# A six-stage graph network on one core: turned-row copies that also read a late weight, and one product issued a step later

## Chip, core and metric

One core of a Trainium2 chip runs the whole kernel. The metric is the device time of one execution in microseconds (us). The matrix engine is called PE, its weight loads PEld, the vector engine DVE, the scalar engine ACT, the general-purpose engine POOL, and SP issues the transfers (DMA).

## The reference, cut to what matters

Input is `x` (3327 x 256) and a 0/1 matrix `adj` (3327 x 3327). Six masked softmax attentions follow one another; each later one reads the rows of the one before.

```python
x = _layernorm(x + L0(x, adj))        # cosine attention          -> layer "0"
x = _layernorm(x + L1(x, adj))        # GAT, elu                  -> layer "1"
x = _layernorm(x + L2(x, adj))        # query-key attention, elu  -> layer "2"
h = x @ W0                            # L3: three GAT layers      -> "3a", "3b", "3c"
h = _gat_layer(h, adj, W1, a1); h = _gat_layer(h, adj, W2, a2); h = _gat_layer(h, adj, W3, a3)
x = _layernorm(x + h)

def _gat_layer(h, adj, W, a):
    Wh = h @ W
    e = jax.nn.leaky_relu(Wh @ a[:F] + (Wh @ a[F:]).T, ALPHA)
    att = jax.nn.softmax(jnp.where(adj > 0, e, NEG_INF), axis=1)
    return jax.nn.elu(att @ Wh)
```

The kernel multiplies the attention weights by `h` first and by `W` afterwards, so each finished block of rows has to be turned (transposed) and multiplied by a 256 x 256 matrix.

## The kernel before, in words

Rows are cut into 26 tiles of 128 (`NT = 26`). Queries are handled in seven blocks: blocks 0 to 5 hold 512 rows (four tiles), and block 6 holds only 256 (two tiles). Block 6 is called the half-wide block here, and block 5 is `b == NB - 2`, the one in front of it.

The main loop runs over layers, blocks and 26 steps `j`. A step takes one tile of weights `e` (128 keys x 512 or 256 queries), which ACT and DVE made some steps earlier (`Gat.weights`, L657 and L668; five buffers hold `e`), and multiplies it with the 128 x 257 rows of values, once for each tile `k` of the block: `po[k] += e[:, k]' * V[j]` (L1405; in the last block of layer 3c, L1390). `po` are PSUM banks, five in all, of which a full block uses four and a half-wide block two. So the fourth tile of block 0 takes the bank in which tile 0 of the half-wide block before was summed, and its first product cannot start before ACT has read that bank (L1026).

The rows of a finished block are completed by the generator `finish(L, b, pos)`, advanced one stage in each step of the next block. In the GAT layers it scales the rows (L1022, L1025 on DVE, L1026 on ACT) and calls `turn`: ACT splits the float rows into 16-bit planes (L834), a transposing DMA writes `turned` (L837), the generator then yields `turn_steps(L, b)` times, and DVE copies the two halves back into float order as `pT4` (two 128 x 1024 16-bit copies for a block of four tiles, L844). In block 5 each tile of `pT4` is then multiplied by the layer's matrix (`pproj`, L1062), followed by elu on ACT and DVE (L1075 to L1091). Block 5 is finished while the half-wide block runs.

Engines work through their own instructions in order. The order is written by hand only in the first four steps; afterwards a scheduler orders each engine's instructions, starting from the program's order. A yield more in a generator therefore moves the instructions after it by a step or less, or not at all.

In the last block of layer 3c (`end` in the loop) the two tiles are done one after the other, all 26 products of the first and then of the second; `finish_last` completes each (L1204 to L1256), while `finish` of block 5 runs beside it (its normalised rows `o4`, L1118, and their stores, L1128). After the last product there is one more `finish_last` chain on PE, ACT and DVE, and a store.

Of the kernel before, what the change touches and what calls it, by code (L numbers as in the profile page):

```python
# [8 lines left out]
F32 = mybir.dt.float32  # L9
# [5 lines left out]
ALU = mybir.AluOpType  # L15
# [4 lines left out]
P = 128  # L20
# [13 lines left out]
def gnn_stack(ctx: ExitStack, tc: tile.TileContext, a: dict, N: int, out: bass.AP):  # L34
# [8 lines left out]
    nc = tc.nc  # L43
    NT = (N + P - 1) // P
    NP = NT * P
    NB = (NP + CH - 1) // CH
# [6 lines left out]
    def tiles_of(b):  # L53
        return range(4 * b, min(4 * b + 4, NT))
# [4 lines left out]
    cols = ctx.enter_context(tc.tile_pool(name="cols", bufs=2))  # L59
# [6 lines left out]
    def bank(name):  # L66
# [4 lines left out]
    start = tc.manual_schedule(  # L71
        engines={engines.PE, engines.Activation, engines.DVE, engines.Pool}
    )
# [9 lines left out]
    n = 8  # L83
# [9 lines left out]
    for k in range(4):  # L93
# [5 lines left out]
    V = [  # L99
        [big.tile([P, D + 1], F32, name=f"v{i}_{t}") for t in range(NT)]  # L100
        for i in range(2)
    ]
# [195 lines left out]
    def load_x(g):  # L298
        for t in tiles_of(g):
            nc.sync.dma_start(V[0][t][:, :D], a["x"][t * P : (t + 1) * P, :])  # L300
# [382 lines left out]
    def strassen(L, b):  # L683
        return L.key == "2" or (L.key == "0" and 0 < b < NB - 1)
# [139 lines left out]
        return z[:, : 2 * q]  # L824


    def turn(x4, n, out, steps=3):

        half = "p k (n t) -> p t k n"
        pl = work.tile([P, 4, 2, D], U16, tag="x4k", name="planes", bufs=2)
        for t in range(2):
            nc.scalar.copy(pl[:, :n, t, :], x4[:, :n, :].bitcast(U16).rearrange(half, t=2)[:, t])  # L834
        yield
        tr = work.tile([P, 16, P], U16, tag="stage", name="turned", bufs=4)
        nc.sync.dma_start_transpose(  # L837
            out=tr[:, : 4 * n, :], in_=pl[:, :n].rearrange("p k t n -> p (k t n)")
        )
        for _ in range(steps):  # L840
            yield
        trv = tr[:, : 4 * n, :].rearrange("p (k t h) i -> p t k h i", t=2, h=2)
        for t in range(2):
            nc.vector.tensor_copy(out(t), trv[:, t])  # L844
        yield

    def turn_steps(L, b):

        if L.key == "1":
            return 5 if b == NB - 2 else 3  # L850
        return 7 if b == NB - 2 else 4

# [79 lines left out]
    def finish(L, b, pos):  # L934
# [4 lines left out]
        n = len(ts_)  # L939
# [71 lines left out]
        else:  # L1011
# [15 lines left out]
            if L.key in x_d:  # L1027
                x4 = work.tile([P, 4, D], F32, tag="stage", name="x4", bufs=4)
# [6 lines left out]
            es, pTs = {}, {}  # L1035

            if L.key != "2":
                pT4 = work.tile([P, 4, 2, P], F32, tag="x4k", name="pT4", bufs=2)
                yield from turn(
                    p4,  # L1040
                    n,
                    lambda t: pT4[:, :n].bitcast(U16).rearrange(
                        "p k h (i t) -> p t k h i", t=2
                    )[:, t],
                    turn_steps(L, b),
                )
                pTs = {k: pT4[:, k] for k in range(n)}
                if b < NB - 2:
                    c4 = work.tile([P, 4, D], F32, tag="x4k", name="c4", bufs=2)
                    yield from projected4(pT4, w[L.w], c4)  # L1050
# [55 lines left out]
        if not L.hidden:  # L1106
# [29 lines left out]
            if L.key == "1":  # L1136
# [8 lines left out]
                for k, t in enumerate(ts_):  # L1145
                    pm = bank("pv")
                    for h in range(2):
# [4 lines left out]
                            start=(h == 0),  # L1152
                            stop=(h == 1),
# [122 lines left out]
    def advance():  # L1276
        while pending:
            try:
                next(pending[0])
                return  # L1280
            except StopIteration:
                pending.popleft()
# [8 lines left out]
    steps = [(L, b, j) for L in layers for b in range(NB) for j in range(NT)]  # L1291
    made = deque()
# [45 lines left out]
    def make_to(n):  # L1338
        nonlocal upto
        while upto < n:  # L1340
            make(upto)
            upto += 1

    for s, (L, b, j) in enumerate(steps):
        last = L.key == "3c"
        end = last and b == NB - 1

        if last and b == NB - 2 and j > 10:
            extra += 1
        first = L.key == "0" and b == 0  # L1350
        if j == 0:
            wo, no = (CH, 4) if strassen(L, b) else (D + 1, len(tiles_of(b)))
            pos = [ps_o.tile([P, wo], F32, tag="po", name="po") for _ in range(no)]
        if first:

            if j == 0:
                load_x(1)
                load_xT(2)
            elif j % 4 == 2 and j < 20:
                load_x((j + 6) // 4)  # L1360
            elif j % 4 == 3 and j < 16:
                load_xT((j + 9) // 4)
        make_to(s + LA + 1 + extra)
        if first:
            if j < 2:
                next(q1)
                if j == 1:
                    next(q1, None)
            elif j == 2 or j % 4 == 1 and j < 18:
                prep = keys0(max(2, (j + 7) // 4))  # L1370
            next(prep, None)
            if j == 4:
                next(prep, None)
        if L.key == "0" and b < NB - 1:

            at = 10 if b == 0 else 3
            if j == at:
                load_xT(b + 1)
            elif j == at + 3:
                kprep = queries0(b + 1)  # L1380
            if j >= at + 3:
                next(kprep, None)
        es = None if end else made.popleft()
        if es is not None:
            gate[0] = es[0] if isinstance(es, tuple) else es
        if end:

            k, h = divmod(2 * j, NT)
            for i in (h, h + 1):
                nc.tensor.matmul(  # L1390
                    pos[k],
                    made[i][:, k * P : (k + 1) * P],
                    V[1][i],
                    start=(i == 0),
                    stop=(i == NT - 1),
                )
            if j == 0:
                xm = fetch_last()
            if j == NT // 2 - 1:
                ends.append(finish_last(pos[0], xm, 0))  # L1400
            if ends:
                next(ends[0], None)
        elif not strassen(L, b):
            for k in range(len(pos)):
                nc.tensor.matmul(  # L1405
                    pos[k],
                    es[:, k * P : (k + 1) * P],
                    V[L.i % 2][j],
                    start=(j == 0),
                    stop=(j == NT - 1),  # L1410
                )
        elif j % 2:
            products(pos, b, j // 2, es, V[L.i % 2])
        if s == 3:
            start.__exit__(None, None, None)
        if L.key == "0" and j == NT - 1 - LA:
            sum_adj(b)
        if first and 9 <= j < 18:
            combine("0", j - 6, V[0], es)
        elif first and 20 <= j < 24:  # L1420
            combine("0", (j - 21) % (NT // 2), V[0], es)
        advance()
        if L.key == "0" and b < NB - 1:
            if j == 8:
                masks[b + 1] = new_mask(b + 1)
        elif j == 8 and not (last and b == NB - 1):
            nb = (b + 1) % NB
            masks[nb] = fetch_mask(nb)
        if (b, j) == (1, 0):

            if L.key == "1":
                setup = setup3("3b", 2, "w_l0_wqk")
            elif L.key == "3a":
                setup = setup3("3c", 3, "w_l1_w")
        if b >= 1 and j % 3 == 1:
            next(setup, None)
        nl, nb = (L, b + 1)
        if nb == NB:
            nl, nb = (None if last else layers[L.i + 1]), 0
        begin = 2 if last and b == NB - 2 else 14  # L1440
        if L.is_gat and (b, j) == (0, 22):
            sum_weights(w[L.w])
        if j == (25 if L.key == "1" else 22) and not end:
            while pending:
                advance()
        if nl is not None and nl.key != "0":
            if j == begin:
                pre = ahead(nl, nb)
            if j >= begin:
                next(pre, None)  # L1450
        if j == NT - 1:
            if b == 0 and not last:
                nl = layers[L.i + 1]
                L.sum = Sum()
                if nl.is_gat:
                    if nl.key == "1":
                        while "row_1" not in w:
                            next(setup)
                    nl.gat = Gat(nl.key)
                    L.gat_next = nl.gat  # L1460
            if end:
                pending.append(finish_last(pos[1], xm, 1))
            else:
                pending.append(finish(L, b, pos))
            advance()
# [65 lines left out]
```

## Time and profile before

| | |
|---|---|
| median of three runs | 2361.19 us (2360.8 to 2361.67) |
| the profiled execution | 2362.33 us, of which the span is 2360.6 us |
| PE busy | 2336.8 us, 99% of the span |
| DVE busy | 1661.3 us, 70% |
| ACT busy | 1222.2 us, 52% |
| chain that ended last | PE 94%, DVE 3%, ACT 1%, DMA 1% |

The chain is the sequence of work that released the last instruction, followed backwards. A share of 94% for PE means that the time is PE's own work, together with what PE had to wait for. An idle DVE or ACT costs nothing in itself.

### The profile page before, as it was taken

The page shows a single profiled execution, that of the slowest core. Times are in us where ns is not written, and L with a number is a line of the kernel's source. Part 1 is how long each engine was busy: PE and PEld are TensorE (multiplying, and loading weights), DVE is VectorE, ACT ScalarE, POOL GpSimd, SP SyncE. Part 2 cuts the span into 40 slices and gives each one's busy share as a digit, 9 for nine tenths or more (in the row PEclk, how much of TensorE's full clock was granted, in tenths as well). Part 3 has the DMA queues.
Part 4 walks back from the last instruction along what each step waited for, and adds up shares of the span by engine and source line. Part 5 has one row for each costly group of instructions (what it writes and reads, how often), then busy time and mean ns, then how long its engine had stood idle before and what let it go on. Part 6 is the DMA issues. An engine that isn't in the chain of part 4 may idle for free.

```text
span 2360.6 us, 33869 instructions
## 1 busy us (share of the span) xinstructions
PE 2336.8 (99%) x12205; PEld 1916.7 (81%) x12205; DVE 1661.3 (70%) x4481; ACT 1222.2 (52%) x1979; POOL 38.2 (2%) x156
## 2 busy tenths in 40 slices
PE   9999999999999999999999999999999999999997
PEld 7788888888888777767767798888888888888886
DVE  7789999867777667566566686666656666666675
ACT  4667777755555422222222255555655555655554
POOL 0000001000000000000000000000000000000000
PEclk9999999999999999999999999999999999999998
DMA  8655566423222322212212221211211111132211
GB/s 274 187 190 185 171 196 193 151 74 83 74 84 60 104 54 88 79 54 88 74 50 73 81 86 50 74 52 26 76 47 43 43 60 52 43 98 70 61 51 39
DMA packets 147292, 214.71 MB, mean 91 GB/s; under 512 B 76093, under 2 KB 101172, under 8 KB 142516
## 3 DMA queue, kind: packets, MB, share of 16 engines
q1 hardware_dynamic: 146852, 212.28, 29.4%
q8 instruction: 96, 1.57, 0.3%
q14 instruction: 72, 0.59, 0.1%
q10 hardware_dynamic: 272, 0.26, 0.0%
HBM read 167.53 MB, written 28.19 MB: 83 GB/s over the span
## 4 chain that ended last, share of the span: by engine, by line
PE 94%; DVE 3%; ACT 1%; DMA 1%; issue 1%; POOL 0%; POOLq 0%; SPq 0%; DVEq 0%
PE po L1405 48%; PE po L779 20%; PE ps L563 12%; PE ps L492 6%; PE pproj L890 3%; PE pv L1148 1%; PE pgq L522 1%; ACT re L657 1%; DMA turned<-planes 1%; PE po L1390 1%; PE pk L353 1%; PE pq L317 0%; DVE e L668 0%; PE pproj L1062 0%; DVE v L668 0%
## 5 line engine op out<-in xcount | busy, mean ns | idle before, releaser
L1405 PE MATMUL po<-v,e 128*128 128x257 f32 x5616 | 1248.6, 381 | 1.5 <-ACT p L1026 1.3
L1405 PEld LDWEIGHTS po<-v,e 128*128 128x128 f32 x5616 | 1057.7, 190 | 165.3 <-issue 9.3
L657 ACT ACTIVATE re<-u,nrh,th 128x512 f32<-128x512 f32 (+1 forms) x728 | 555.4, 780 | 486.7 <-DVE e L668 481.0
L668 DVE SCALAR_TENSOR_TENSOR e<-re,rh,mask 128x512 f32<-128x512 f32 (+1 forms) x702 | 500.9, 718 | 333.6 <-PE po L1405 282.5
L563 PE MATMUL ps<-gT,ft 128*128 128x512 f32 (+1 forms) x728 | 307.4, 563 | 0.0
L571 ACT ACTIVATE ex<-ps,off 128x512 f32<-128x512 f32 (+1 forms) x182 | 119.1, 656 | 356.2 <-PE ps L563 354.5
L779 PE MATMUL po<-tsums,ssum 128*128 128x128 f32 (+1 forms) x1794 | 249.3, 275 | 0.0
L477 DVE SCALAR_TENSOR_TENSOR e<-ex,mask 128x512 f32<-128x512 f32 (+1 forms) x182 | 118.6, 652 | 163.5 <-ACT ex L571 162.6
L779 PEld LDWEIGHTS po<-tsums,ssum 128*128 128x128 f32 x1794 | 224.5, 192 | 0.7 <-ACT y L982 0.3
L563 PEld LDWEIGHTS ps<-gT,ft 128*128 128x128 f32 x728 | 132.0, 190 | 114.5 <-issue 111.7
L779 PEld LDWEIGHTS po<-v,e 128*128 128x128 f32 x1196 | 169.3, 191 | 67.2 <-issue 53.1
L779 PE MATMUL po<-v,e 128*128 128x129 f32 x1196 | 182.3, 275 | 0.0
L505 ACT ACTIVATE ex<-ps,rq 128x512 f32<-128x512 f32 (+1 forms) x183 | 118.9, 652 | 117.6 <-PE ps L492 107.7
L492 PE MATMUL ps<-ft,ft 128*128 128x512 f32 (+1 forms) x312 | 142.5, 561 | 0.0
L506 DVE SCALAR_TENSOR_TENSOR e<-ex,mask 128x512 f32<-128x512 f32 (+1 forms) x183 | 116.9, 644 | 33.6 <-ACT ex L505 32.7
L449 DVE CUSTOM_DVE_ANT_0 acc<-acc,stage 128x1024 uint16<-128x1024 uint16 (+1 forms) x168 | 108.8, 648 | 12.2 <-DMA stage<-in_adj_a 8.8
L779 PE MATMUL po<-v,ssum 128*128 128x128 f32 x598 | 92.2, 275 | 0.0
L779 PE MATMUL po<-tsums,e 128*128 128x128 f32 x598 | 92.1, 275 | 0.0
L436 ACT ACTIVATE mask<-pos 128x1024 uint8<-128x1024 bf16 (+1 forms) x87 | 86.3, 992 | 2.1
L435 ACT ACTIVATE pos<-stage 128x1024 bf16<-128x1024 int32 (+1 forms) x87 | 85.6, 983 | 1.2 <-DVE e L506 1.2
L779 PEld LDWEIGHTS po<-v,ssum 128*128 128x128 f32 x598 | 79.4, 192 | 0.1
L779 PEld LDWEIGHTS po<-tsums,e 128*128 128x128 f32 x598 | 79.3, 192 | 0.0
(290 smaller groups left out, 1895.2 us busy)
## 6 DMA issues: line engine op xcount, KB each, us to landing
mask<-mask_d SPq DMA_DIRECT2D x30, 1664.0 KB
stage<-in_adj_a SPq DMA_DIRECT2D x78, 512.0 KB
tsums<-t_d SPq DMA_DIRECT2D x152, 256.5 KB
mask_d<-mask SPq DMA_DIRECT2D x6, 1664.0 KB
u<-s_d SPq DMA_DIRECT2D x24, 256.0 KB
xT<-in_xT SPq DMA_DIRECT2D x10, 512.0 KB
mask<-mask_d SPq DMA_DIRECT2D x5, 832.0 KB
t_d<-tsums SPq DMA_DIRECT2D x14, 256.5 KB
```

The costliest lines, as they stand in the source:

```text
L436: nc.scalar.activation(mask(b, j, 2), t_[:, : 2 * wd], AF.Sign)
L449: nc.vector.tensor_tensor(acc, acc, st[:, h * wd : (h + 1) * wd], ALU.add)
L477: nc.vector.scalar_tensor_tensor(e[:, :wd], t_[:, :wd], 0.0, mask(b, j), ALU.add, ALU.mult)
L492: nc.tensor.matmul(ps[:, :wd], FT[j // 4][:, 0, (j % 4) * P : (j % 4 + 1) * P], FT[b][:, 1, :wd], start=True, stop=True,)
L505: nc.scalar.activation(t_[:, c], ps[:, c], AF.Exp, scale=rq[:, j : j + 1])
L506: nc.vector.scalar_tensor_tensor(e[:, c], t_[:, c], 0.0, mask(b, j)[:, c], ALU.add, ALU.mult)
L563: nc.tensor.matmul(ps[:, :wd], FT[j // 4][:, h, (j % 4) * P : (j % 4 + 1) * P], g[:, h, :wd], start=(h == 0), stop=(h == 1),)
L571: nc.scalar.activation(t_[:, :wd], ps[:, :wd], AF.Exp, bias=off, scale=1.0 / D**0.5)
L657: nc.scalar.activation(t_[:, :wd], self.u[b][:, :wd], AF.Relu, bias=self.nrh[:, j : j + 1], scale=self.th[:, j : j + 1],)
L668: nc.vector.scalar_tensor_tensor(e[:, :wd], t_[:, :wd], self.rh[:, j : j + 1], mask(b, j), ALU.add, ALU.mult,)
L779: nc.tensor.matmul(o, x, y, start=(p == 0 and g not in banks[:i]), stop=(p == NT // 2 - 1 and g not in banks[i + 1 :]),)
L1405: nc.tensor.matmul(pos[k], es[:, k * P : (k + 1) * P], V[L.i % 2][j], start=(j == 0), stop=(j == NT - 1),)
```

## The change

Two things are changed.

First, in `turn`, when it is called for `pT4` of block 5 in layers 1, 3a and 3b (`late`), the two copies become additions of a per-partition value `nought`, which is 0 and is computed from the newest weights tile that exists. The copies thereby depend on those weights. The number of yields ahead of the copies goes from 5 to 6 in layer 1 and from 7 to 9 in layer 3c; it stays 7 in 3a and 3b. Layer 3c keeps plain copies.

Second, in block 0 of layers 3b and 3c, the first product of the fourth tile (step 0) is issued in step 1, between the third and the fourth product of that step.

```diff
-    def turn(x4, n, out, steps=3):
+    def turn(x4, n, out, steps=3, late=False):
...
         trv = tr[:, : 4 * n, :].rearrange("p (k t h) i -> p t k h i", t=2, h=2)
-        for t in range(2):
-            nc.vector.tensor_copy(out(t), trv[:, t])
+        if late:
+
+            e = next(m for m in reversed(made) if m is not None)
+            nought = cols.tile([P, 1], F32, tag="nought", name="nought")
+            nc.vector.tensor_scalar(nought, e[:, :1], 0.0, None, ALU.is_lt)
+            for t in range(2):
+                nc.vector.tensor_scalar(out(t), trv[:, t], nought, None, ALU.add)
+        else:
+            for t in range(2):
+                nc.vector.tensor_copy(out(t), trv[:, t])
         yield
     def turn_steps(L, b):
         if L.key == "1":
-            return 5 if b == NB - 2 else 3
-        return 7 if b == NB - 2 else 4
+            return 6 if b == NB - 2 else 3
+        if b == NB - 2:
+            return 9 if L.key == "3c" else 7
+        return 4
...
                     turn_steps(L, b),
+                    b == NB - 2 and L.key != "3c",
                 )
...
         elif not strassen(L, b):
-            for k in range(len(pos)):
+            todo = [(es, j, k) for k in range(len(pos))]
+
+            if L.key in ("3b", "3c") and b == 0:
+                if j == 0:
+                    held = todo.pop()
+                elif j == 1:
+                    todo.insert(3, held)
+            for e, i, k in todo:
                 nc.tensor.matmul(
                     pos[k],
-                    es[:, k * P : (k + 1) * P],
-                    V[L.i % 2][j],
-                    start=(j == 0),
-                    stop=(j == NT - 1),
+                    e[:, k * P : (k + 1) * P],
+                    V[L.i % 2][i],
+                    start=(i == 0),
+                    stop=(i == NT - 1),
                 )
```

In the order of instructions that the scheduler makes of the changed program, each engine's row of instructions is the old one with these differences:

- Layers 1, 3a and 3b, DVE: the two copies stand where they stood, behind the weights tile of step 12. `nought` stands two or three weights tiles ahead of them. Of the elu work behind them, the first operation comes one weights tile later.
- Layers 1, 3a and 3b, PE: the first `pproj` stands where it stood, between the two products of step 10. In layer 1 the second `pproj` now comes behind the second product of step 10 instead of in front of it, and the third and fourth come one step later. In 3a and 3b nothing moves.
- Layer 3c, last block, PE: each `pproj` of block 5 comes four products later: the first behind product 23 of the first tile instead of product 19, the fourth behind product 9 of the second tile instead of product 5, and so behind the projection of `finish_last` for the first tile. ACT and DVE follow; the four `o4` and their stores come behind the store of the first `olast`.
- Block 0 of 3b and 3c, PE: the held product moves as written. ACT: the `u` of the next block (L649) comes ahead of two `re` (L657) instead of behind them.

## The prediction

> **What bounds the kernel now.** I read the page first: busy time and the chain that ended last.
>
> ```profile
> PE 2336.8 (99%) x12205; PEld 1916.7 (81%) x12205; DVE 1661.3 (70%) x4481; ACT 1222.2 (52%) x1979; POOL 38.2 (2%) x156
> PE 94%; DVE 3%; ACT 1%; DMA 1%; issue 1%; POOL 0%; POOLq 0%; SPq 0%; DVEq 0%
> ```
>
> PE is idle for only 2360.6 - 2336.8 = 23.8 us. The change takes away no product, so it can win only from that idle time. Next come PE's waits (line waited for: us in total, times, longest).
>
> ```profile
> PE pproj L1062 <- DVE pT L844: 4.8, 4, 1.5
> PE pasum L464 <- DVE af L460: 2.0, 2, 1.6
> PE po L1405 <- ACT p L1026: 1.3, 2, 0.7
> ```
>
> The change touches the first and the third row. In the timeline of PE the four waits on pT are 0.71 us (layer 1, before 786.42), 1.05 (3a, before 1689.96), 1.54 (3b, before 2008.74) and 1.50 (3c, before 2326.50). Those on p are 0.66 (block 0 of 3b) and 0.65 (block 0 of 3c). Together 6.1 us. Another 13.2 us lie behind the last product work (PE ends at 2347.4), where the last rows are completed and stored.
>
> What ends the waits on pT is seen in the timeline of 3b, and of 3c:
>
> ```profile
> 2007.33 1.35 DVE L844 COPY pT<-turned 128x1024 uint16<-128x1024 uint16 x2 [1.70 <-DMA turned<-planes]
> ...
> 2008.74 1.13 PE L1062 MATMUL pproj<-w_l_w,pT 128*128 128x256 f32 x4 [1.53 <-DVE pT L844]
> ...
> 2325.00 1.35 DVE L844 COPY pT<-turned 128x1024 uint16<-128x1024 uint16 x2 [1.79 <-DMA turned<-planes]
> 2326.50 1.10 PE L1062 MATMUL pproj<-w_l_w,pT 128*128 128x256 f32 x4 [1.50 <-DVE pT L844]
> ```
>
> DVE stands before the copies and waits for the transposing DMA (1.70 and 1.79 us; 0.87 in layer 1, 1.20 in 3a). The copies then take 1.35, and PE follows within 0.15 us. So two things set the end of this wait: when the DMA lands, and how long the copies last. The change alters the second and leaves the first. The rows that price copies, by shape (busy us, mean ns of one | idle before):
>
> ```profile
> L844 DVE COPY pT<-turned 128x1024 uint16<-128x1024 uint16 x48 | 32.9, 740 | 17.9 <-DMA turned<-planes 17.9
> L1118 DVE TENSOR_SCALAR v<-y,st,rstd 128x256 f32<-128x256 f32 x52 | 18.3, 409 | 0.3
> L1079 DVE TENSOR_SCALAR z<-c 128x256 f32<-128x256 f32 x40 | 9.0, 288 | 0.3
> L432 DVE TENSOR_SCALAR mask<-stage 128x1024 uint8<-128x1024 int32 x4 | 2.7, 686 | 0.0
> L537 DVE TENSOR_REDUCE gm<-gT 128x2 f32<-128x1024 f32 x6 | 7.3, 1219 | 13.9 <-ACT gT L529 13.9
> ```
>
> L1079 and L1118 handle the same 128x256 floats in SBUF. The one with a constant takes 288 ns, the one with per-partition scalars 409: 121 ns more for 256 elements, 0.47 ns an element.
>
> **Held product, 3b and 3c.** Before, the fourth tile's first product waits until ACT has read the bank. Now three products of step 1 go ahead of it: PE runs took 6.66 us for 30 such instructions and 4.93 us for 22, so a product (two instructions) costs 1.73 / 4 = 0.43 us and three 1.29 us, against waits of 0.66 and 0.65. Both waits go: -1.3 us. What covers it is the weights tile of step 1, which must exist; DVE's weights wait mostly for PE to free a buffer (the row below), so they run ahead. The tile of step 0 is released 1.3 us later, and with five buffers its successor is wanted only about four steps (6.9 us) on.
>
> ```profile
> DVE e L668 <- PE po L1405: 282.5, 345, 1.4
> ```
>
> The `u` of the next block, now two `re` earlier on ACT, delays those by its 0.70 us. Its DMA was issued at 1702.30 and it would run at about 1711.9, 9.6 us later, where the transposes landed within 4 to 5; the weights behind have the slack just named. Cost 0.
>
> **Tail, layer 3c.** The first `pproj` stands four products later, 1.72 us of PE work. PE reaches it at 2325.00 + 1.72 = 2326.72, and pT is complete at 2326.35. The wait of 1.50 us goes. What is late next? The fourth `pproj` used to start at 2334.59. Counting PE's work up to product 9 (2338.04 before, less 1.50, less one `pproj` of 0.86), it now starts at 2335.7. That is 1.1 us later, and all of block 5's normalisation follows on DVE, queued ahead of the second `plast` copy (L1204) that starts the last chain. Before, DVE needed from that tile's L1082 (2336.06) to the end of `olast` (2343.46) 7.40 us; of this, L1229 to L1234 (0.48 + 0.42 + 0.42 + 0.43) now run earlier, so DVE is free at about 2337.2 + 5.65 = 2342.9. PE's last product ends at 2345.14 - 1.50 = 2343.64. The margin is 0.8 us; if that cover is gone, the last chain starts late by what is missing, at worst most of the 1.5. The four `o4` stores, moved on SP behind the first `olast` store, are issued in 1.80 us, some 7 us ahead of the last store. The DMA queue is otherwise empty there. I take -1.5 us.
>
> **Restart.** Four `pproj` instructions after a wait take 1.13 or 1.10 us, others 1.03: each wait removed saves 0.1 us more. Three waits: -0.3 us.
>
> **Copies in layers 1, 3a, 3b.** In the changed order the copies stay behind the weights of step 12, and the first `pproj` stays between the products of step 10. The DMA lands when it did. So the waits of 0.71, 1.05 and 1.54 us stay. What changes is the copy itself: an addition with a per-partition scalar. No such row on 16-bit data exists. From below: it costs what the copy costs (740 ns; L432, a TENSOR_SCALAR with a constant, does 1024 elements in 686), so 0. From above: the copy loses its rate as L1118 does against L1079, 0.47 ns x 1024 = 0.48 us more, 1.22 us each; L537, the slowest row for 1024 elements, is also 1.22. I take the upper end, since L1118 is the only SBUF row with per-partition scalars. The pair runs nearly back to back, so pT is 0.97 us later. DVE was waiting for the DMA and PE for DVE, so nothing hides it: 3 x 0.97 = +2.9 us.
>
> [...]
>
> `nought` itself, 128x1: L708 is the same operation at 148 ns; it stands two or three weights ahead of the copies and falls into DVE's idle time (0.87 to 1.70 us before the copies): 0. Behind the copies wait the weights of steps 13 and 14, 0.97 us later; PE holds the products of steps 10 to 12 and a `pproj` or two, over 2.5 us of work, so it does not run dry. The elu one weights tile later, and layer 1's second to fourth `pproj` later, reorder PE work without a wait: PE showed no gap over 0.3 us from there to the end of that layer.
>
> **Sum.** -1.3 - 1.5 - 0.3 + 2.9 = -0.2 us. The profiled execution took 2362.33 us (span 2360.6 and 1.7 around it), 1.14 above the median. Against its own time it would become 2362.1; against the median of 2361.19, 2361.0.
>
> **The rivals.**
>
> *The addition keeps the copy's rate.* L1118 has two operations and two scalars, and its lost rate may be due to either; L432 and L1079 show that TENSOR_SCALAR as such can be fast. Then -1.3 - 1.5 - 0.3 = -3.1 us: 2358.1. [...]
>
> *Slower: the 16-bit addition with a stride-2 output runs at half of the single rate.* Then each takes about 2 x 1.22 = 2.4 us, the pair 3.4 us longer than the copies: 3 x 3.4 - 3.1 = +7.1 us, 2368.3. It decides from an extra 2.6 us a pair on ((4.7 + 3.1) / 3), where the kernel is over 0.2% slower. Against it: no DVE row in the trace needs over 1.22 us for 1024 elements.
>
> *The tail gives nothing back.* DVE's normalisation holds up the last chain and the 1.5 us return: +1.3 us, 2362.5. Against it stands the margin of 0.8 us.
>
> *The change does what its dependence suggests: all six waits go.* -6.1 - 0.6 = -6.7 us and copies at no extra cost, 2354.5. Against it: the place of copies and `pproj` is the same, and the DMA lands as late (2007.33, when PE was already waiting since 2007.20).
>
> **How the numbers follow.** Forecast as summed 0.67, its own range 2360.2 to 2361.8 (DMA landing and pitch); copy's rate kept 0.16; tail gives nothing 0.06; half rate 0.06; all waits gone 0.05. The range, 2357.7 to 2362.6, takes in the first three. A difference of 0.2%, 4.7 us, is about what a measurement of this kernel can tell from no change. Faster by more: 0.05. Slower by more: 0.06. Within: 0.89.
>
> **What would show it.** In the changed profile, the six wide copies should be TENSOR_SCALAR of about 1.22 us; PE's wait for pT should come three times, about 1.7, 2.0 and 2.5 us, 6.2 in all; the wait on p (L1026) should be gone, and the wait in the last block too, with the last plast copy (L1204) still released by PE. Copies of 0.74 us would make the second case true; a wait before the last chain on something else than PE, the fourth.

## The result, and the profile after

The changed kernel takes 2358.08 us (median of 22 runs, 2356.71 to 2359.34); the kernel before took 2361.22 in as many runs on the same chip. The ratio is 0.9986, with a 95% interval of 0.998 to 0.9992: 3.1 us are gone, where the forecast was 0.2. The number fell inside the range of 2357.7 to 2362.6 but below the forecast's own 2360.2 to 2361.8, and it is that of the first rival, the addition that keeps the copy's rate (2358.1).

The profiled execution took 2358.10 us, its span 2356.2. The two profiled spans differ by 4.4 us, more than the medians; 1.2 of this lies in the first matmuls of the program, which are the same in both kernels. So the waits below are compared one by one, and the spans are not. First the page of the changed kernel, busy time and chain:

```profile
PE 2334.6 (99%) x12205; PEld 1915.6 (81%) x12205; DVE 1661.7 (71%) x4484; ACT 1222.4 (52%) x1979; POOL 39.9 (2%) x156
PE 96%; DVE 2%; DMA 1%; ACT 0%; issue 0%; POOL 0%; SPq 0%; DVEq 0%
```

PE has the same 12205 instructions; DVE has three more, the three `nought`. PE's part of the chain rose from 94% to 96%, ACT's 1% is gone. The waits of PE in the changed kernel (line waited for: us in total, times, longest):

```profile
PE pproj L1073 <- DVE pT L849: 2.7, 3, 1.1
...
PE pn L545 <- DVE g L542: 0.7, 1, 0.7
```

The row for `p` (it would be L1036 now) is gone, and so is the fourth wait for pT: both as forecast. The three that remain are 2.7 us in all, not the 6.2 forecast. And there is a row that the forecast did not have, 0.7 us for `g`. The price of the copies, in the groups of DVE instructions (busy us, mean ns of one | idle before):

```profile
L852 DVE COPY pT<-turned 128x1024 uint16<-128x1024 uint16 x42 | 28.7, 739 | 14.1 <-DMA turned<-planes 14.1
L849 DVE TENSOR_SCALAR pT<-turned,nought 128x1024 uint16<-128x1024 uint16 x6 | 4.4, 792 | 2.8 <-DMA turned<-planes 2.8
L847 DVE TENSOR_SCALAR nought<-e 128x1 f32<-128x1 f32 x3 | 0.5, 153 | 0.1
```

The addition with a per-partition scalar takes 792 ns beside 739 for the plain copy, where 1220 was forecast. The timeline of 3a and of the two places that were shown of before, 3b and 3c:

```profile
1689.83 1.13 PE L1073 MATMUL pproj<-w,pT 128*128 128x256 f32 x4 [1.07 <-DVE pT L849]
...
2001.05 2.06 SPq L837 DMA_TRANSPOSE turned<-planes  x1
...
2005.45 1.48 DVE L849 TENSOR_SCALAR pT<-turned,nought 128x1024 uint16<-128x1024 uint16 x2 [0.85 <-DMA turned<-planes]
2006.98 1.13 PE L1073 MATMUL pproj<-w_l_w,pT 128*128 128x256 f32 x4 [0.81 <-DVE pT L849]
...
2322.32 1.37 DVE L852 COPY pT<-turned 128x1024 uint16<-128x1024 uint16 x2 [1.79 <-DMA turned<-planes]
2323.89 1.05 PE L1073 MATMUL pproj<-w_l_w,pT 128*128 128x256 f32 x4
```

In 3b the pair of copies grew from 1.35 to 1.48 us, yet PE's wait fell from 1.54 to 0.81, because DVE waited for the transposes only 0.85 us instead of 1.70: the copies start 4.40 us after the issue of the transposes, where they started 5.24 us after it before. That is something the change does not speak of at all. In 3c PE reaches `pproj` 0.20 us after pT is complete and waits for nothing; the four instructions take 1.05 us instead of 1.10. The end of the tail:

```profile
2338.38 1.38 DVE L1129 TENSOR_SCALAR o<-y,st,rstd 128x256 f32<-128x256 f32 x4
2340.78 0.29 DVE L1215 COPY plast<-po 128x128 f32<-128x128 f32 x1 [1.01 <-PE po L1401]
```

DVE ends the normalisation of block 5 at 2339.76 and then waits 1.01 us for PE's last product. The cover that was forecast at 0.8 us is there.

### The profile page after: what moved, and what is told of

The parts are those of the page before. It is cut to its first block, busy times and chain, and to the rows that moved or that the text cites. A ratio compares the mean times of both kernels' runs of the same rounds, so it can differ in the third digit from the quotient of the medians.

```text
span 2356.2 us, 33876 instructions
## 1 busy us (share of the span) xinstructions
PE 2334.6 (99%) x12205; PEld 1915.6 (81%) x12205; DVE 1661.7 (71%) x4484; ACT 1222.4 (52%) x1979; POOL 39.9 (2%) x156
## 4 chain that ended last, share of the span: by engine, by line
PE 96%; DVE 2%; DMA 1%; ACT 0%; issue 0%; POOL 0%; SPq 0%; DVEq 0%
PE po L1423 50%; PE po L779 20%; PE ps L563 12%; PE ps L492 6%; PE pproj L900 3%; PE po L1401 1%; PE pv L1159 1%; PE pgq L522 1%; PE pproj L1073 1%; DMA stage<-in_adj_a 1%; PE pk L353 0%; PE pq L317 0%; DVE e L506 0%; PE pn L329 0%; DMA turned<-planes 0%
## 5 line engine op out<-in xcount | busy, mean ns | idle before, releaser
L657 ACT ACTIVATE re<-u,nrh,th 128x512 f32<-128x512 f32 (+1 forms) x728 | 555.1, 780 | 486.1 <-DVE e L668 480.0
```

Source lines behind the costliest of these rows:

```text
L657: nc.scalar.activation(t_[:, :wd], self.u[b][:, :wd], AF.Relu, bias=self.nrh[:, j : j + 1], scale=self.th[:, j : j + 1],)
```

## The experiments

Each kernel ran beside the kernel before on the same chip; differences are against the median of the kernel before measured beside it. Waits are those of the profiled execution. "The tie" is the dependence of the late copies on the newest weights, through `nought`.

**e1, the price of a scalar by itself.** One instruction of each kind, twelve times in a row, without any waits between them: the 128x256 floats with constants, with one and with two scalars, then the 16-bit copy and its variants. The instructions are shortened here.

```diff
+    tensor_scalar(y, f, 0.0, None, max)         # L33   constant, one operation
+    tensor_scalar(y, f, 0.5, 2.0, sub, mult)    # L35   constants, two operations
+    tensor_scalar(y, f, a0, None, add)          # L37   one scalar, one operation
+    tensor_scalar(y, f, a0, 2.0, sub, mult)     # L39   one scalar, two operations
+    tensor_scalar(y, f, a0, a1, sub, mult)      # L41   two scalars (as the old L1118)
+    tensor_copy(pT, turned)                     # L43
+    tensor_scalar(pT, turned, 0.0, None, add)   # L45   16 bits, constant
+    tensor_scalar(pT, turned, a0, None, add)    # L47   16 bits, one scalar (the change)
+    tensor_scalar(pT, turned, a0, a1, add, add) # L49   16 bits, two scalars
```

> No part of the network is computed: the kernel copies x to the output and runs nine forms of TENSOR_SCALAR and COPY on DVE, twelve of each, on tiles in SBUF of the shapes disputed. It tells what made L1118 slow (409 ns for 128x256 floats, against 288 ns at L1079) when the 16-bit addition with a per-partition scalar kept its rate (792 ns in the changed kernel, copy 740). Theory A, two per-partition scalars cost the double rate and one does not: floats with a constant 285, with two operations and constants 285, with one scalar about 335, one scalar and two operations 335, two scalars 405; 16-bit with one scalar 790, with two scalars about 1220. Theory B, the second operation costs it: two operations slow (405) even with constants. Theory C, floats with any per-partition scalar are slow (405), 16-bit data are not: one scalar on floats 405, 16-bit with two scalars about 800.

The groups of DVE instructions in e1:

```profile
L49 DVE TENSOR_SCALAR pT<-turned,s 128x1024 uint16<-128x1024 uint16 x12 | 9.0, 860 | 0.0
L47 DVE TENSOR_SCALAR pT<-turned,s 128x1024 uint16<-128x1024 uint16 x12 | 8.4, 796 | 0.0
L43 DVE COPY pT<-turned 128x1024 uint16<-128x1024 uint16 x12 | 7.5, 726 | 0.0
L45 DVE TENSOR_SCALAR pT<-turned 128x1024 uint16<-128x1024 uint16 x12 | 7.5, 724 | 0.0
L41 DVE TENSOR_SCALAR y<-f,s 128x256 f32<-128x256 f32 x12 | 4.0, 422 | 0.0
L39 DVE TENSOR_SCALAR y<-f,s 128x256 f32<-128x256 f32 x12 | 3.3, 362 | 0.0
L37 DVE TENSOR_SCALAR y<-f,s 128x256 f32<-128x256 f32 x12 | 3.2, 360 | 0.0
L35 DVE TENSOR_SCALAR y<-f 128x256 f32<-128x256 f32 x12 | 2.5, 299 | 0.0
L33 DVE TENSOR_SCALAR y<-f 128x256 f32<-128x256 f32 x12 | 2.5, 298 | 0.0
```

Read the means by pairs. On 256 floats: no scalar 298, one 360, two 422. On 1024 16-bit elements: 724, 796, 860. Each scalar adds 62 to 72 ns to the instruction, nearly the same for 256 floats as for 1024 16-bit elements, and on the floats a second operation adds nothing (298 and 299, 360 and 362). So it is a fixed cost and no lost rate. Size and type change together in these two groups; the rows of the kernel before that are shown further down have two sizes of one type and say the same. None of the expectations had that: two scalars on 16 bits come out at 860, neither at the rate of the copy nor at the lost one.

**e2, e3 and e4, the parts one by one.** e2 has the held product alone, e3 the nine yields of 3c alone, e4 the late copies of 1, 3a and 3b (with six yields in layer 1) alone. Against the changed kernel:

```diff
 e2 and e3, both:
-            return 6 if b == NB - 2 else 3
+            return 5 if b == NB - 2 else 3
-                    b == NB - 2 and L.key != "3c",
+                    False,
 e2 and e4:
-            return 9 if L.key == "3c" else 7
+            return 7
 e3 and e4:
-            if L.key in ("3b", "3c") and b == 0:
+            if False:
```

> The kernel before with the held product alone (block 0 of layers 3b and 3c). By the prediction's step both waits of 0.65 us on p (L1026) go and with them 0.1 us each of restart: -1.5 us, and nothing else moves. Rival: the product held keeps its tile of weights 1.3 us longer and DVE falls behind, so the waits come back in front of a later product: 0 us, with a wait on e in the profile.

> The kernel before with nine yields instead of seven in layer 3c alone. By the prediction's step the wait of 1.5 us in front of the first pproj of the last block goes, with 0.1 us of restart: -1.6 us, and the last plast copy is released by PE with DVE idle some 0.8 to 1.0 us ahead of it. Rival: the normalisation, 1.1 us later, delays the last chain and the gain is under 0.5 us.

> The kernel before with the tied copies alone (layers 1, 3a, 3b; six yields in layer 1). Theory A: the addition of 792 ns instead of 740 puts 0.12 us into each of three waits on pT, and layer 1's order puts 0.7 us in front of the pn product (L545): +0.4 + 0.7 = +1.1 us. Theory B: the tie brings a gain of its own (the changed kernel measured 3.1 us less, where hold and tail explain 3.1 only if nothing is lost elsewhere): 0 to -1 us. The prediction's own term was +2.9 us.

Measured: e2 2359.04 us, 2.2 below the kernel before by the medians and 1.7 by the ratio (0.9993, 0.9984 to 1.0001); e3 2359.51, 1.7 below (0.9993, 0.9984 to 1.0002); e4 2361.53, 0.3 above (1.0001, 0.9992 to 1.001). Each of these intervals includes no change at all, so the rows have to carry it. Waits of PE in e2, in e3 and in e4:

```profile
PE pproj L1073 <- DVE pT L852: 4.8, 4, 1.6
```

```profile
PE pproj L1073 <- DVE pT L852: 3.3, 3, 1.5
...
PE po L1423 <- ACT p L1036: 1.3, 2, 0.7
```

```profile
PE pproj L1073 <- DVE pT L849: 2.9, 3, 1.1
...
PE pproj L1073 <- DVE pT L852: 1.5, 1, 1.5
PE po L1423 <- ACT p L1036: 1.3, 2, 0.7
...
PE pn L545 <- DVE g L542: 0.7, 1, 0.7
```

In e2 the row of `p` is gone and the four waits for pT are 4.8 us as before; in e3 one of the four is gone (3.3 us in three) and `p` is still 1.3. So these two parts do what was forecast, each without touching the other's wait. e4 keeps the waits of 3c and of `p`, carries the new one for `g`, and its three waits for pT are 2.9 us, where they were 0.71 + 1.05 + 1.54 = 3.3 before the copies became longer. The late copies are worth nothing: what they lose at `g` they find again at the transposes of 3b.

**e5 and e6, what made the transposes of 3b come earlier.** e5 is e4 with `nought` in a buffer that was there already, so that nothing in memory moves. e6 is the kernel before with a new buffer for a `nought` that nobody reads, so that everything moves and nothing is tied.

```diff
 e5, against e4:
-            nought = cols.tile([P, 1], F32, tag="nought", name="nought")
+            nought = cols.tile([P, 1], F32, tag="z1", name="nought")
 e6, against the kernel before:
+        if n == 4 and steps == 7:
+            nought = cols.tile([P, 1], F32, tag="nought", name="nought")
+            nc.gpsimd.memset(nought, 0.0)
```

> The tied copies alone, as in the run before, but nought lies in a column that another tile already has, so that no buffer moves: with a tile of its own, the working buffers (planes and turned among them) all lie 64 bytes further on in SBUF. Open is why in layer 3b the copies start 4.4 to 4.6 us after the issue of the transposing DMA with the tie and 5.24 to 5.26 without. Theory A, the place in SBUF: 5.2 us again, wait on pT in 3b 1.54 + 0.12 = 1.66 us. Theory B, the tie or the instructions that it adds to DVE: 4.4 to 4.6 us and a wait of 0.8 to 1.0 us.

> The kernel before with an unused column tile of the size of nought (set by POOL, read by nobody), in layers 3a and 3b; copies plain and untied. All working buffers lie 64 bytes further on, as in the changed kernel. Theory A, the place in SBUF: in 3b the copies start 4.4 to 4.6 us after the issue and the wait on pT is 0.7 to 0.9 us. Theory B, the tie: 5.2 us and 1.54 us as before.

These are single runs, 2363.04 and 2361.30 us, which say nothing by themselves; the rows do. Copies and first `pproj` of 3b in e5, and below them in e6:

```profile
2007.84 1.47 DVE L849 TENSOR_SCALAR pT<-turned,nought 128x1024 uint16<-128x1024 uint16 x2 [0.93 <-DMA turned<-planes]
2009.37 1.13 PE L1073 MATMUL pproj<-w_l_w,pT 128*128 128x256 f32 x4 [0.89 <-DVE pT L849]
```

```profile
2006.15 1.35 DVE L847 COPY pT<-turned 128x1024 uint16<-128x1024 uint16 x2 [1.69 <-DMA turned<-planes]
2007.56 1.13 PE L1065 MATMUL pproj<-w_l_w,pT 128*128 128x256 f32 x4 [1.53 <-DVE pT L847]
```

In e5 the copies of 3b start 4.47 us after the transposes are issued and PE waits 0.89; in e6 5.23 and 1.53, as in the kernel before (5.24 and 1.54). The place in memory is not the cause; it is the tie or the instruction that comes with it. The records of the transfers offered a candidate, which e9 tests: the packets of queue q14 (of the kind "instruction" in the page, 72 packets and 0.59 MB, 8192 bytes each) fall in different places among the transposes' packets, 3.87 us after the issue in 3b of the kernel before and 0.62 in the changed kernel. They are read here as the fetch of the program itself.

**e7 and e8, the wait for `g`, and a later projection.** e7 is the changed kernel with five yields in layer 1. e8 has also nine yields in 3a and 3b, and one yield less ahead of the shift for the next layer.

```diff
 e7 and e8:
-            return 6 if b == NB - 2 else 3
+            return 5 if b == NB - 2 else 3
 e8 also:
-            return 9 if L.key == "3c" else 7
+            return 9 if L.key == "3c" else 9
-                yield
+                if not L.hidden:
+                    yield
```

> The changed kernel with five yields in layer 1 as before instead of six; the rest unchanged. Theory: the wait of 0.7 us in front of the pn product (L545), which came with the change, comes from the one step that layer 1's rows are completed later; with five yields it goes, 0.7 us against the changed kernel, about -3.8 us against the kernel before. Rival: it comes from the later copies (pT 0.1 us later) and stays; no difference from the changed kernel, -3.1 us.

> The changed kernel with five yields in layer 1, and in layers 3a and 3b nine yields instead of seven with one yield less behind the rows (ahead of the shift), so that the first pproj stands behind both products of step 11, three products (1.29 us) later. By the theory that DMA landing and copies set the end of these waits and only PE's place matters, the waits of 1.07 and 0.81 us go, with 0.1 us of restart each: 2.1 us against the version with five yields, about -5.9 us against the kernel before. Rival: the scores of the last rows come later, the next layer's first weights wait, and PE stands at the start of 3b and 3c: gain under 1 us, with a new wait there.

e7: 2358.46 us, 3.3 below the kernel before (0.9986, 0.9977 to 0.9995). The row of `g` is gone, so the sixth yield had made that wait; but the wait for pT in 3a rose from 1.07 to 1.69, and nothing is left of the gain. e8: 2358.40, 3.3 below (0.9985, 0.9976 to 0.9994). Waits of PE in e8:

```profile
PE po L1424 <- DVE e L668: 1.9, 2, 1.0
...
PE pproj L1073 <- DVE pT L849: 1.2, 2, 0.8
```

The waits for pT shrink to 1.2 us, and the first products of 3b and 3c now wait for their weights, 0.97 and 0.96 us. The rival in the expectation came true: what is put off in block 5 is missing at the start of the next layer.

**e9 and e10, the fetch of the program.** e9 is the kernel before with six memsets of one column at the start of DVE's program: every later DVE instruction stands six places further on, and nothing else changes. e10 is the changed kernel without the tie.

```diff
 e9, against the kernel before:
+    for _ in range(6):
+        nc.vector.memset(part[:, :1], 0.0)
 e10, against the changed kernel:
-                    b == NB - 2 and L.key != "3c",
+                    False,
```

> The kernel before with six more one-column memsets (128x1) at the very start of DVE's program. No instruction of the six stages is changed, no buffer is moved, and nothing is tied; only the place of every later DVE instruction in the program is six instructions further on. In the records of the transfers the program itself is fetched in pieces of 8192 bytes, and in 3b of the kernel before such a piece comes about 4.1 us after the issue of the transposing DMA, just as its packets end; the copies then start 5.24 us after the issue, where 4.4 is seen without a fetch. Theory (a fetch that falls behind the transposes delays them or DVE): the fetch comes earlier, copies of 3b start 4.3 to 4.7 after the issue, and PE's wait for pT in 3b is 0.7 to 1.0 us where it was 1.54. Rival (the later copies come from the tie, the 128x1 operation or the place of the copies among the weights): 5.24 and 1.54 stay. The time of the kernel: 2360.5 by the theory, 2361.3 by the rival, which one look cannot tell apart; the rows decide.

> The changed kernel with plain copies in every layer (no tie, no nought), the yields and the held product as in the changed kernel. The copies stand where they stood. If the scalar costs its fixed 65 ns in each of six copies, 0.35 us come back. Theory of the fetch: without the three additional 128x1 operations DVE's program is as long as before up to 3b, so the fetch falls behind the transposes of 3b again, copies start 5.2 after the issue and the wait is about 1.5 us: net +0.3 us against the changed kernel, 2358.1 to 2358.7. Rival (the fetch has nothing to do with it): the wait of 3b stays 0.8 or sinks to 0.7, and the time is 0.35 us below that of the changed kernel, 2357.7.

e9 took 2360.26 us in its single run. The timeline of 3b in e9, and below it that of e10 (copies and `pproj` of 3a, then copies of 3b):

```profile
2000.90 2.40 SPq L839 DMA_TRANSPOSE turned<-planes  x1
2005.24 1.36 DVE L846 COPY pT<-turned 128x1024 uint16<-128x1024 uint16 x2 [0.80 <-DMA turned<-planes]
2006.66 1.13 PE L1064 MATMUL pproj<-w_l_w,pT 128*128 128x256 f32 x4 [0.64 <-DVE pT L846]
```

```profile
1687.35 1.36 DVE L852 COPY pT<-turned 128x1024 uint16<-128x1024 uint16 x2 [1.71 <-DMA turned<-planes]
1688.77 1.13 PE L1073 MATMUL pproj<-w,pT 128*128 128x256 f32 x4 [1.54 <-DVE pT L852]
...
2005.21 1.35 DVE L852 COPY pT<-turned 128x1024 uint16<-128x1024 uint16 x2 [1.68 <-DMA turned<-planes]
```

Six memsets at 0 us move the copies of 3b from 5.24 to 4.34 us after the issue and PE's wait from 1.54 to 0.64. Taking the tie out, e10, puts 3b back to 5.23 and a wait of 1.52, and 3a from 1.07 to 1.54. The time of e10 is 2358.76, 2.4 below the kernel before (0.999, 0.9981 to 0.9999). The rival, that the fetch has nothing to do with it, falls on both rows. The fetch itself is seen in a view of the DMA share by slices of 0.05 us (last two columns: mean busy share of the DMA engines, GB/s; a packet is put into the slice in which it starts). The kernel before in 3b, from 3.81 us after the issue on:

```profile
2005.90:2005.95 0.05, 0.05 (x2) 0.04 (x1) 0.00 (x0) 0.05 (x1) 0.00 (x0) 1.00 0.07 15
2005.95:2006.00 0.05, 0.05 (x2) 0.04 (x1) 0.00 (x0) 0.05 (x1) 0.00 (x0) 1.00 0.39 164
2006.00:2006.05 0.05, 0.05 (x2) 0.05 (x1) 0.00 (x0) 0.05 (x1) 0.00 (x0) 1.00 0.00 0
```

and e9, 0.60 us after the issue:

```profile
2001.50:2001.55 0.05, 0.05 (x2) 0.03 (x1) 0.05 (x1) 0.05 (x1) 0.00 (x0) 1.00 0.47 164
```

164 GB/s for 0.05 us are 8.2 KB, one piece of the program. In the kernel before it comes where the transposes run out, in e9 before they have begun. The table has it from the records of single packets, in us after the issue of the transposes, on the zero of the timeline; on it the piece that the expectation of e9 puts at 4.1 starts at 3.87.

| kernel, layer | fetch of 8192 bytes | last transposing packet ends | copies start |
|---|---|---|---|
| before, layers 1 and 3c | none | 3.82, 3.80 | 4.42, 4.31 |
| e9, 3b | 0.61 to 0.99 | 3.84 | 4.34 |
| changed, 3b | 0.62 to 1.06 | 3.83 | 4.40 |
| changed, 3a | 1.89 to 2.20 | 4.04 | 4.66 |
| before, 3a | 3.95 to 4.26 | 3.95 | 4.75 |
| before, 3b | 3.87 to 4.18 | 4.19 | 5.24 |
| e10, 3a | 3.88 to 4.19 | 4.20 | 5.25 |
| e10, 3b | 3.85 to 4.16 | 4.17 | 5.23 |

A fetch that starts just ahead of the last transposing packets (before in 3b, e10 in both layers) costs 0.8 to 0.9 us: the last of them ends 0.01 us behind the fetch, some 0.35 late, and the copies start 1.05 us behind it instead of 0.5. Where the fetch starts just as that packet ends (before, 3a), the copies are 0.35 to 0.45 late.

DVE could also have been standing there for want of its own next instructions. The landings speak against it: the trace records sixteen for each of these transfers, and in the cases named here the copies start 0.02 us behind the last. In 3b of the kernel before, fifteen are in at 4.35 us after the issue and the sixteenth at 5.22; in e10, 4.41 and 5.23 in 3a, 4.34 and 5.21 in 3b. In 3b of e9 fifteen are in at 4.27 and the sixteenth at 4.32. So DVE waits for the transfer, and a fetch just ahead of its end made one of its sixteen landings late.

**e11, five yields and eight.** The changed kernel with five yields in layer 1 and eight in 3a and 3b, so that the first `pproj` comes one product later.

```diff
-            return 6 if b == NB - 2 else 3
+            return 5 if b == NB - 2 else 3
-            return 9 if L.key == "3c" else 7
+            return 9 if L.key == "3c" else 8
```

> The changed kernel with five yields in layer 1 and eight in 3a and 3b. In layer 1 PE's wait of 0.7 us for g (pn, L545) should go, as it went with five yields. In 3a and 3b the first pproj stands behind both products of step 10 instead of between them: one product, 0.43 us, later. Theory (the landing of the transposes sets the end of the wait): PE's waits for pT of 1.07 and 0.81 become 0.64 and 0.38, if the fetch falls as in the changed kernel, and the time is 0.7 + 0.9 = 1.6 us below it at best, 2356.5; with a fetch behind the transposes of 3a, as five yields in layer 1 had it (copies 5.28 after the issue), 0.6 less of that, 2357.1. Rival (what comes later in block 5 comes later at the start of the next layer, as with nine yields): new waits for e at the start of 3b and 3c, about 0.4 us each, and the time stays within 0.5 us of that of the changed kernel.

2358.41 us, 2.7 below the kernel before (0.9989, 0.998 to 0.9998). The wait for `g` is gone, but the fetch of 3a starts 3.84 us after the issue (copies 5.29 after the issue, wait 1.25), and the first products of 3b and 3c wait 0.5 us each for `e`. Here too the rival came true.

**e12, what gained, and the fetch moved.** The kernel before with the held product, the nine yields of 3c and the six memsets of e9; no tie and no sixth yield.

```diff
 against the changed kernel:
+    for _ in range(6):
+        nc.vector.memset(part[:, :1], 0.0)
-            return 6 if b == NB - 2 else 3
+            return 5 if b == NB - 2 else 3
-                    b == NB - 2 and L.key != "3c",
+                    False,
```

> The two parts that gained (held product, nine yields in 3c), the kernel before in all else (plain copies, five yields in layer 1), and six one-column memsets at the start of DVE's program, as in e9. Theory (gains add, the scalars and the sixth yield cost what was found, the fetch is moved by the memsets as in e9): -1.5 for the held product, -1.6 for the tail, and for the fetch what e9 showed, PE's waits for pT of 1.05 and 1.54 in 3a and 3b becoming 0.81 and 0.64, so -1.1: 4.2 us below the kernel before, 2356.9, and 1.1 below the changed kernel; no wait for g (L545). Rival (the fetch is one of many small shifts, and what is won in 3a and 3b is lost elsewhere): the rows of 3a and 3b as above, but a new wait or a fetch in another place, and the time within 0.5 us of that of the changed kernel, 2358.1.

2356.73 us, 4.0 below the kernel before (ratio 0.9982, 0.9973 to 0.9991). The largest waits of PE in e12:

```profile
PE pasum L466 <- DVE af L462: 2.5, 2, 1.9
PE pproj L1075 <- DVE pT L854: 2.1, 3, 0.8
```

The first row belongs to the loading of `adj` at the start and is 1.5 us in the profile of e3 and 2.6 in that of the changed kernel. The waits for pT are 0.68, 0.63 and 0.84, and there is none for `p`, `g` or `e`. The fetch starts 0.66 us after the issue in 3a and 0.87 in 3b. The intervals of e12 and of the changed kernel overlap, and the two were not measured side by side; by the rows e12 has 1.3 us less of waits.

**All of them by waits.** The sum of PE's waits for pT, `p`, `g` and `e`, and its difference to the 6.1 us of the kernel before, beside the measured times:

| kernel | waits, us | difference | time measured |
|---|---|---|---|
| e2, held product | 4.8 | -1.3 | -2.2 |
| e3, tail | 3.3 + 1.3 = 4.6 | -1.5 | -1.7 |
| e4, late copies | 2.9 + 1.5 + 1.3 + 0.7 = 6.4 | +0.3 | +0.3 |
| changed kernel | 2.7 + 0.7 = 3.4 | -2.7 | -3.1 |
| e7 | 3.5 | -2.6 | -3.3 |
| e8 | 1.2 + 1.9 = 3.1 | -3.0 | -3.3 |
| e10, no tie | 3.7 + 0.7 = 4.4 | -1.7 | -2.4 |
| e11 | 2.6 + 1.0 = 3.6 | -2.5 | -2.7 |
| e12 | 2.1 | -4.0 | -4.0 |

The single runs e5, e6 and e9 are left out. Four groups of rows follow the times within 0.9 us through nine kernels, though each measured difference is itself known only to 1.4 to 2.1 us either way. The measured gain is a little larger than that of the waits in most rows; the shorter restarts behind a removed wait go that way, but do not make up all of it.

## Why the prediction was right or wrong

*Held product, -1.3.* Right: the row of `p` is gone in the changed kernel and in e2, with nothing in its place. The cover named, a weights tile that is ready, held.

*Tail, -1.5.* Right: the wait is gone, the last chain is still released by PE (L1215 behind L1401), and the margin came out at 1.0 us for 0.8. The third rival falls with it.

*Restart, -0.3.* Not measured apart. The `pproj` of 3c is 1.05 us for 1.10, half of what was put down for a wait; the waits alone give 0.4 us less than the medians, into which it would fit.

*Copies, +2.9.* This is the term that was mis-sized, and it decided between the forecast and its rival. Measured: 0.12 us a pair (1.48 for 1.36), 0.35 in all. The failed step is "0.47 ns an element": the difference of two rows of one size, 121 ns at 256 elements, was read as a rate, though one size cannot tell a rate from a fixed cost. By e1 it was two scalars of 62 ns each. Multiplied by 1024 the difference became 0.48 us. Read as a fixed cost, the same two rows would have given 60 ns for the one scalar of the new copy, and the sum -2.7. The choice of the upper end, "since L1118 is the only SBUF row with per-partition scalars", leaned on the row that had the scalar and not on L432, which had the element count. It is also not so: L1255 has the same form and takes 412 ns. And the second size stood in the profile before, in rows that read PSUM:

```profile
L1079 DVE TENSOR_SCALAR z<-pproj 128x256 f32<-128x256 f32 x12 | 5.1, 424 | 5.6 <-ACT elu_e L1075 5.3
L1229 DVE TENSOR_SCALAR ylast<-pproj,ri 128x256 f32<-128x256 f32 x2 | 1.0, 480 | 1.3 <-ACT elu_e L1226 1.3
L388 DVE TENSOR_SCALAR ft<-pk,rk 128x128 f32<-128x128 f32 x2 | 0.6, 346 | 0.0
L1204 DVE COPY plast<-po 128x128 f32<-128x128 f32 x2 | 0.6, 288 | 1.7 <-PE po L1390 1.7
```

L1229 and L388 have one per-partition scalar, L1079 and L1204 none: 56 ns more at 256 elements, 58 at 128. A cost per element would have halved. In e1 the 16-bit TENSOR_SCALAR with a constant takes 724 ns beside 726 for the copy, and one scalar makes it 796. The rival of the half rate, 2.4 us each, falls too.

*"The DMA lands when it did."* Wrong in 3b: copies 4.40 us after the issue instead of 5.24, worth 0.85 us of wait there, and 1.0 over the three layers (3.3 before, 0.35 for the copies, 2.7 after). By e9, e10 and the landings this comes from where a fetch of the program falls, not from the dependence that the change adds. Such a cause could not have been read out of the diff; but the spread, 4.3 to 5.2 us for the same transfer in one profile, could have been put into the range as a term with two ends.

*Layer 1, "reorder PE work without a wait".* Wrong by 0.7 us: the second to fourth `pproj` later, and with them the normalisation on DVE, put `g` behind PE's need of it. e7 takes the sixth yield away, and the row goes. PE had no wait there before (none from 787 to 850 us in the profile before), but the slack behind that was not measured.

So -1.3 - 1.5 - 0.3 + 0.35 + 0.7 - 1.0 = -3.05, and 3.1 were measured. That the first rival's number was met to 0.1 us is in part luck: two terms that neither the forecast nor the rival had, +0.7 and -1.0, nearly cancel. The last rival, all waits gone, falls: the copies and `pproj` stayed where they were, and three waits with them.

## What to carry to other kernels

A price taken from two rows of one size is a difference, not a rate: before it is multiplied by another size, find a third row that tells a fixed cost from a cost per element, or carry both. Where the waits that a change touches are under 1 us, take the change apart and add up the waits by row: nine kernels here whose times lie within 4.8 us of each other are told apart by four rows. And when a wait for a transfer changes without a reason in the diff, look at what other transfers ran beside it, the program's own fetch included (0.8 to 0.9 us here), before crediting the edit.

## What the runs showed of the hardware that was not expected

A per-partition scalar cost DVE 62 to 72 ns an instruction, for 256 floats as for 1024 16-bit elements, and a second operation in the same instruction, measured on the floats, nothing (298 and 299, 360 and 362 ns in e1). In the kernels themselves the difference is 53 to 58 ns (792 and 739 in the changed kernel, 480 and 424, 346 and 288 before).

The fetch of the program in pieces of 8192 bytes held up a transposing DMA and the copies that wait for it: in 3a and 3b of the runs here it was 5.23 to 5.29 us from issue to copy where it starts at 3.82 to 3.88, 4.70 to 4.75 at 3.91 to 3.95, 4.61 to 4.73 at about 1.9, and 4.30 to 4.58 where it starts before 0.9 or not at all. Six instructions of one column at the start of DVE's program moved it in 3b, 2000 us later, from 3.87 to 0.61 us after the issue (e9). The page has the packets of the kind "instruction" on queues of their own (q8 and q14).

What stays open: why one landing comes 0.8 to 0.9 us behind the other fifteen when the last packets are only some 0.35 us late, and what sets the place of the fetch exactly. The trace does not name the engine whose program a piece on q14 holds; that it is DVE's is read from its moving with DVE's six more instructions in e9, and is not shown otherwise. The changed kernel and e7 have the same number of DVE instructions up to 3a, and there the fetch starts at 1.89 us in the one and at 3.83 in the other.
